# A perceiver kernel: the order of the mixer's loads, the early exponential and the place of two key pieces

## The chip, the cores and the metric

The kernel runs on one core of a Trainium2 chip. The metric is the device time of one execution in microseconds (us). The profile is that of one execution; its times are counted from the start of the profiled span, which is a little shorter than the execution that it belongs to.

## The reference

The kernel is a network of four layers on a latent `x` of 2 x 256 rows of 256 values, with a context `ctx_1024` of 2 x 4096 rows of 256. Each step is a residual of the layer-normed latent:

```python
x = x + _L0_xattn_ref(_layernorm(x), ctx_1024, ...)   # attention over the context
x = x + _L0_attn_ref(_layernorm(x), ...)              # self-attention, 16 heads of 16
x = x + _L0_ffn_ref(_layernorm(x), ...)
x = x + _L1_xattn_ref(_layernorm(x), ctx_1024, ...)   # 16 heads of 64 over the context
x = x + _L1_attn_ref(_layernorm(x), ...)              # the mixer: a scan with W_in, a conv, W_dt, W_out
x = x + _L1_ffn_ref(_layernorm(x), ...)               # int8 weights
x = x + _L2_xattn_ref(ctx_1024, _layernorm(x), ...)   # a long convolution
x = x + _L2_attn_ref(_layernorm(x), ...)
x = x + _L2_ffn_ref(_layernorm(x), ...)               # attention, then routed experts
x = x + _L3_xattn_ref(_layernorm(x), ctx_1024, ctx_1024, ...)
x = x + _L3_attn_ref(_layernorm(x), ...)
x = x + _L3_ffn_ref(_layernorm(x), ...)               # experts, one a row
```

Three parts matter here. The mixer starts with a projection by `W_in`:

```python
zxbcdt = hidden_states @ W_in
z, x, Bm, Cm, dtr = jnp.split(zxbcdt, [...], axis=-1)
```

Each self-attention has a softmax over its scores. And layer 3's attention has one key and one value of 16 for all heads, over the whole context:

```python
kvp = c @ w_kv
k, v = (kvp[..., :D_HEAD], kvp[..., D_HEAD:])
attn_score = jnp.einsum('bhid,bjd->bhij', qh, k) / np.sqrt(D_HEAD)
```

## The kernel before

The 512 rows of the latent lie in four tiles of 128 partitions (`NT` = 4, `x` is 128 x 4 x 256). The layers are methods of one class, emitted one after the other by `perceiver`; a scheduler then sets the order of each engine's instructions from data dependences and what is free, except where a block is wrapped in `in_order(engines)` (L339): there every instruction of a named engine is made to follow the one before it in the program. Memory comes from pools that are opened and closed in the order of the layers. A pool that is opened may lie over one that was closed, and its tiles then wait for the old one. PSUM banks are such a pool too, with the tags mm, tr, acc and dec (`banks`, called in `perceiver` for each layer); a tag with fewer buffers than tiles hands them out in the order in which the tiles are made. Weights come from a pool `wp` of four slots by `weight` (L315 and on), all loaded on SP's queue.

**The start of the mixer.** `l1_attn` (L1464) opens a pool `l1a`. Its first tile is `win` (128 x 2 x 1728 fp32, 1728 KB), loaded at L1474, then the weights wdt and wout, three spread matrices (L1481) and the loads of the next stage in `conv_load` (L1655). `dt2` and `neg_a` (L1486) are small preparations on DVE and ACT; `to_T` (L427) normalizes and transposes `x`; `project` multiplies slices of `win` with it. The tiles `low` and `high` (8 KB per partition each) come later in the same pool. Before the mixer stands the layer-1 attention, which ends with its output matmuls (L1234, `ps_mm` from w_l1x_wo). In the wait for its last sums TensorE works on pieces of layer 3's keys (`ahead_in_drain`, L971 and on).

**Keys ahead of their layer.** A piece of layer 3's keys is two matmuls for 512 context rows (`ahead_key`, two steps of a generator; each fp32 matmul is two records of L971 in the trace, 128 x 512). `ahead_out` (L951) evicts a piece into a tile `ahead_t` (L959 on ACT) and writes it to DRAM as `ahead_k` (L963, 256 KB) from the same engine. `fill_from` and `fill(n)` (L1053) advance such a generator by n steps. `ahead_fetch` (L945) loads what the pieces need: the weights `ahead_l3x_wk`, `ahead_l3x_wv` and the context piece `ahead_piece`. It is called in `perceiver` when the stage int8_and_conv begins. The last two pieces are `ahead_behind`: their context lies in a pool `behind` whose tile `ahead_t` has one buffer, and they are the pieces of the boundary between layers 2 and 3.

**The boundary before layer 3.** `l2_ffn` ends with `experts_in_turn` (L2245): the experts' matmuls, a gather of rows (DVE at L2066) and `bring_back` (matmuls at L359, an addition at L2233). `l3_xattn` then begins with `layernorm` (L373: statistics on DVE, a square root on ACT at L368, the scaling at L384), then the four steps of `fill(4)` and the transposes of `to_T` (L435) in one `in_order(PE)`. The pools of `behind` close after that, and the pool `l3x` with the query's tiles opens. The keys are read back as kT (L2375); `proj_heads` gives qT (L359 with w_l3x_wq); the scores' maxima start with `quad` (L2403) and `mx` (L2407).

**The early exponential.** `self_attention` (L787) is used three times. At L866 it makes a tile `first` and takes an exponential of ones into it, in an `in_order` of PE, DVE and ACT ahead of the loop in which `weights` takes the exponentials of the scores (L840).

Of the kernel before, what the change touches and what calls it, by code (L numbers as in the profile page):

```python
# [11 lines left out]
F32 = mybir.dt.float32  # L12
# [10 lines left out]
P = 128  # L23
# [246 lines left out]
class Perceiver:  # L270
# [518 lines left out]
    def self_attention(self, pool, qT, kT, v, scale, rest=(), fill=None, at=(range(6), range(6, 16), range(16, 22))):  # L789

        nc = self.nc
        z = pool.tile([P, NT, D], F32, name="z")
        with ExitStack() as s:
            one = s.enter_context(self.tc.tile_pool(name="sa_1", bufs=1))  # L800
            pp = s.enter_context(self.tc.tile_pool(name="sa_pt", bufs=14))
            pads = [one.tile([P, 2, 2, P], F32, name=f"mpad{g}") for g in range(4)]
            for pad in pads:
                nc.gpsimd.memset(pad, 0.0)
            zT = [one.tile([P, 4, L], F32, name=f"zTs{b}") for b in range(B)]
            pts, avs = {}, {}

            def maxima(i):

                g, n = divmod(i, 4)  # L810
                b, j = divmod(g, 2)
                rs, t = ((0, 1), (2, 3))[n % 2], n // 2
                lead = pads[g][:, t].rearrange("p c (r w) -> p c r w", w=32)[:, :, :, 0]
                got = [self.bank([P, 2, L]) for _ in rs]
                for c in range(2):
                    for r, ps in zip(rs, got):
                        nc.tensor.matmul(  # L817
                            ps[:, c, :], qT[ts(r, 32), 2 * j + c, ts(2 * b + t, P)], kT[ts(r, 32), 2 * j + c, ts(b, L)],
                            start=True, stop=True,
                        )  # L820
                        yield
                for r, ps in zip(rs, got):
                    nc.vector.tensor_reduce(lead[:, :, r], ps, AX.X, ALU.max, negate=True)

            def weights(i):

                g, n = divmod(i, 4)
                b, j = divmod(g, 2)
                rs, c = ((2, 3), (0, 1))[n % 2], 2 * j + n // 2
                got = [self.bank([P, 2, L], "tr") for _ in rs]  # L830
                for kt in range(2):
                    for r, ps in zip(rs, got):
                        nc.tensor.matmul(  # L833
                            ps[:, kt, :], kT[ts(r, 32), c, ts(2 * b + kt, P)], qT[ts(r, 32), c, ts(b, L)],
                            start=True, stop=True,
                        )
                        yield
                for r, ps in zip(rs, got):
                    pts[c, b, r] = pp.tile([P, 2, L], F32, name="PT", tag="PT")
                    nc.scalar.activation(pts[c, b, r], ps, AF.Exp, scale=scale)  # L840

            def shift(g):
                b, j = divmod(g, 2)
                ps = self.acc([P, 2, 2, P])
                for c in range(2):
                    for t in range(2):
                        nc.tensor.transpose(ps[:, c, t, :], pads[g][:, t, c, :], self.ident)
                q = qT[:, ts(j, 2), ts(b, L)]
                return lambda: nc.vector.tensor_add(q, ps.rearrange("p c t q -> p c (t q)"), q)

            def weigh(g):
                b, j = divmod(g, 2)
                av = self.acc([P, 2, L])
                for c in range(2):
                    for kt in range(2):
                        for r in range(4):
                            h = 4 * (2 * j + c) + r
                            nc.tensor.matmul(
                                av[ts(r, 32), c, :], v[:, 2 * b + kt, h, :], pts[2 * j + c, b, r][:, kt, :],
                                start=kt == 0, stop=kt == 1,  # L860
                            )
                nc.scalar.copy(zT[b][:, ts(j, 2), :], av)

            e = mybir.EngineType
            with self.in_order(e.PE, e.DVE, e.Activation):
                first = self.sm.tile([P, 1], F32, name="first", tag="first")  # L866
                nc.scalar.activation(first, self.ones[:, 0:1], AF.Exp)
                for k in range(16 + 6 + 2):
                    its = []
                    if k < 16:  # L870
                        its.append(maxima(k))
                    if 0 <= k - 6 < 16:
                        its.append(weights(k - 6))
                    then = None
                    if its:
                        self.steps_in_turn(*its)
                    if k < len(rest):
                        rest[k]()
                    for steps, tag, vector in zip(at, ("tr", "acc", "mm"), (False, False, True)):
                        if fill is not None and k in steps:  # L880
                            fill(1, tag, vector)
                    if k % 4 == 0 and 4 <= k <= 16:
                        shift(k // 4 - 1)()
                    if k % 4 == 2 and k >= 10:
                        weigh((k - 10) // 4)
                    if k in (15, 23):
                        b = 0 if k == 15 else 1
                        for t in range(2):
                            self.heads_back(z[:, 2 * b + t, :], zT[b][:, :, ts(t, P)], "acc")
        return z  # L890
# [573 lines left out]
    def l1_attn(self, x):  # L1464
# [5 lines left out]
        with ExitStack() as s:  # L1470
            pool = s.enter_context(self.tc.tile_pool(name="l1a", bufs=1))
            p4 = s.enter_context(self.tc.tile_pool(name="l1a4", bufs=6))
            win = pool.tile([P, KC, 1728], F32, name="win")
            nc.sync.dma_start(win, self.dram["l1a_win"])  # L1474
            wdt = self.weight("l1a_wdt")
            wout = self.weight("l1a_wout")
            mats = {}
            for n in "xbc":
                src = self.dram[f"spread_{n}"]
                mats[n] = pool.tile(list(src.shape), F32, name=f"mat_{n}")  # L1480
                nc.sync.dma_start(mats[n], src)  # L1481
            self.conv_load()
            dt2 = self.sm.tile([P, 4], F32, name="dt2", tag="dt2")
            nc.vector.tensor_scalar_mul(dt2, self.colv("dt_bias"), 2.0)
            neg_a = pool.tile([P, 64], F32, name="neg_a")
# [17 lines left out]
            for k in range(1, 4):  # L1503
                nc.vector.scalar_tensor_tensor(
                    xc, xpad[:, :, k : k + L], self.col("conv_w", k), xc, ALU.mult, ALU.add
                )

            low, high = pool.tile([P, 4, T], F32, name="low"), pool.tile([P, 4, T], F32, name="high")

            def steps_of(j):  # L1510
                ps = self.bank([P, T], "dec")
# [429 lines left out]
    def l2_ffn(self, x):  # L1941
        nc = self.nc
        T = NT * P
        with ExitStack() as s:
# [125 lines left out]
                return add  # L2070

            self.experts_in_turn(unit, n, kept, gather, ways, way, y)
            return y


# [270 lines left out]
    def l3_xattn(self, x, *stacks):  # L2346
# [7 lines left out]


        nc = self.nc
        xn = self.layernorm(x)
        self.fill_from(self.behind_parts)
        with self.in_order(mybir.EngineType.PE):
            self.fill(4)  # L2360
            xnT = self.to_T(xn)
        for stack in stacks:
            stack.close()
        with ExitStack() as s:
# [397 lines left out]
def perceiver(tc, dram, out, col_at, row_at, layers=LAYERS):  # L2762
    with ExitStack() as ctx:
# [6 lines left out]
        for name in layers:  # L2770
            if name == "l0_xattn":
                k.banks(banks, "l0x", 3, 2, 2, 1)
            elif name == "l0_attn":
                banks.close()
                k.banks(banks, "a", 3, 3, 2)
                k.early_open(early)
            elif name == "l1_xattn":

                banks.close()
                early.close()  # L2780
                head.close()
                tern.close()
                k.banks(banks, "l1x", 4, 2, 1, 1)
            elif name == "l1_attn":
                banks.close()
                k.banks(banks, "l1a", 3, 2, 1, 2)
                k.ahead_load(ahead_head)
                k.conv_open(conv)
            elif name == "int8_and_conv":
                banks.close()  # L2790
                k.banks(banks, "l2x", 4, 2, 2)
                k.ahead_fetch()
            elif name == "l2_attn":
                conv.close()
                banks.close()
                k.banks(banks, "c", 3, 3, 2)
                k.l2_keep = keep.enter_context(tc.tile_pool(name="l2f_keep", bufs=1))
                k.ahead_stack, k.behind_stack = ahead, behind
                k.ahead_open(ahead)
            elif name == "l3_xattn":  # L2800

                banks.close()
                k.banks(banks, "l3q", 4, 4, 0)
                k.bank_stack = banks
            elif name == "l3_attn":
                banks.close()
                k.banks(banks, "b", 3, 3, 2)
# [34 lines left out]
```

## Time and profile before

| what | value |
|---|---|
| median of 3 runs | 2532.66 us (2529.35 to 2532.92) |
| the profiled execution | 2533.07 us |
| its span | 2531.3 us |
| mean granted TensorE clock | 0.974 |
| TensorE (PE) busy | 2419.0 us, 96% |
| VectorE (DVE) busy | 1691.5 us, 67% |
| ScalarE (ACT) busy | 1345.3 us, 53% |
| GpSimd (POOL) busy | 911.9 us, 36% |
| DMA | 243.58 MB, 96 GB/s over the span |

The engines are PE (matmul), PEld (its weight loads), DVE, ACT, POOL and SP; a q behind a name is the engine's own queue (semaphores, DMA issues). A line of the timeline has the start, the duration, the engine, the line of the kernel, the operation, out <- in with their shapes, how many instructions were joined, and in brackets how long the engine had stood idle and who released it. The chain of work that ended last is followed back from the last instruction; a window of it lists start, duration and what. In a line of groups, durations are in ns as minimum/median/maximum, then the first and the last start in us.

### The profile page before, as it was taken

To read this page: it belongs to the slowest core of one execution; us is meant where nothing else is said; L and a number is where in the kernel's file an instruction comes from. 1 tells how busy PE (TensorE), PEld (TensorE's weight loads), DVE (VectorE), ACT (ScalarE), POOL (GpSimd) and SP (SyncE) were. 2 spreads that over 40 slices of the span, in tenths; PEclk is the share of its full clock that TensorE was granted. 3 is DMA by queue.
4 is the path that set the end of the run, shared out by engine and by line. 5 is a ranking of instruction groups with operands and counts; after the bars stand their busy time and mean duration, and the time that the engine had idled before them with its cause. 6 is when DMAs were issued, how large, how long until landed. Compare 5 with 4: busy or idle time off the path is not lost.

```text
span 2531.3 us, 51258 instructions
## 1 busy us (share of the span) xinstructions
PE 2419.0 (96%) x20467; PEld 1620.3 (64%) x20469; DVE 1691.5 (67%) x3071; ACT 1345.3 (53%) x2550; POOL 911.9 (36%) x856
## 2 busy tenths in 40 slices
PE   8999999999999999999899989999969999999889
PEld 6865477777766666666533556456926666665678
DVE  5555588888877777777679656444278888845542
ACT  3334576666666666666566323332106777783512
POOL 0420066666655666656459221001101222200010
PEclk9999999999999999999999999989989999998889
DMA  7221433333342222222400102217730000004556
GB/s 298 96 94 69 138 101 93 97 100 99 101 126 68 68 68 69 73 71 85 148 9 1 67 21 96 80 55 279 260 106 2 2 2 2 2 2 167 185 234 216
DMA packets 92637, 243.58 MB, mean 96 GB/s; under 512 B 8072, under 2 KB 23248, under 8 KB 81904
## 3 DMA queue, kind: packets, MB, share of 16 engines
q1 hardware_dynamic: 81088, 219.08, 25.9%
q10 hardware_dynamic: 8784, 13.24, 1.4%
q0 software_dynamic: 2528, 8.00, 0.9%
q8 instruction: 161, 2.64, 0.4%
q14 instruction: 76, 0.62, 0.1%
HBM read 206.87 MB, written 33.42 MB: 95 GB/s over the span
## 4 chain that ended last, share of the span: by engine, by line
PE 88%; DVE 6%; ACT 3%; issue 2%; DMA 1%; DVEq 0%; ACTq 0%; SPq 0%; POOL 0%; POOLq 0%
PE ps_tr L1234 15%; PE ps_mm L359 13%; PE ps_mm L1281 10%; PE acc L1328 9%; PE ps_tr L2462 5%; PE ps_mm L2422 5%; PE ps_tr L2446 5%; PE acc L359 4%; PE ps_tr L359 2%; PE acc L563 2%; PE acc L1611 2%; PE ps_mm L817 2%; PE ps_mm L1234 2%; DVE mx L2407 1%; PE ps_tr L833 1%
## 5 line engine op out<-in xcount | busy, mean ns | idle before, releaser
L1316 POOL TENSOR_TENSOR total<-total,S 128x512 f32<-128x512 f32 x434 | 543.0, 1283 | 227.7 <-ACT S L1305 227.1
L1305 ACT ACTIVATE S<-S 128x512 f32<-128x512 f32 x512 | 304.1, 626 | 209.6 <-DVE S L1302 209.2
L1291 DVE TENSOR_TENSOR most<-ps_mm,most 128x512 f32<-128x512 f32 x448 | 278.1, 683 | 101.0 <-ACT S L1288 101.0
L1302 DVE TENSOR_TENSOR S<-S,ps_dec 128x512 f32<-128x512 f32 x512 | 317.3, 678 | 1.7 <-PE ps_dec L1363 1.7
L2426 DVE TENSOR_REDUCE mx<-ps_mm 128x1 f32<-128x512 f32 x448 | 278.1, 683 | 52.2 <-PE ps_tr L2446 48.2
L1288 ACT COPY S<-ps_mm 128x512 f32<-128x512 f32 x512 | 262.3, 598 | 73.0 <-PE ps_mm L1281 73.0
L2450 ACT ACTIVATE PT<-ps_tr 128x512 f32<-128x512 f32 x476 | 246.8, 601 | 82.4 <-PE ps_tr L2446 79.2
L1234 PEld LDWEIGHTS ps_tr<-w_l1x_wv,ctxT 128*64 128x64 f32 x4096 | 235.5, 137 | 46.3 <-issue 41.7
L1281 PE MATMUL ps_mm<-qT,kT 64*128 64x256 f32 x2048 | 256.6, 389 | 1.8 <-DVE qT L1240 1.8
L1328 PE MATMUL acc<-S,v 128*64 128x256 f32 x2048 | 252.2, 385 | 1.7 <-ACT S L1305 1.0
L1234 PE MATMUL ps_tr<-w_l1x_wv,ctxT 128*64 128x128 f32 x4096 | 248.3, 273 | 0.0
L2446 PE MATMUL ps_tr<-qm,kT 32*128 32x256 f32 x1904 | 240.1, 390 | 0.0
L2422 PE MATMUL ps_mm<-kT,qT 32*128 32x512 f32 x896 | 229.1, 628 | 3.0 <-DVE mx L2407 2.8
L1281 PEld LDWEIGHTS ps_mm<-qT,kT 64*128 64x128 f32 x2048 | 188.5, 186 | 45.5 <-issue 12.0
L1328 PEld LDWEIGHTS acc<-S,v 128*64 128x64 f32 x2048 | 139.5, 136 | 96.3 <-ACT S L1288 33.8
L1234 PE MATMUL ps_tr<-ctxT,w_l1x_wk 128*64 128x512 f32 x800 | 189.6, 593 | 0.0
L2446 PEld LDWEIGHTS ps_tr<-qm,kT 32*128 32x128 f32 x1904 | 172.5, 185 | 16.5 <-issue 6.2
L2471 POOL TENSOR_TENSOR sums<-sums,part 128x256 f32<-128x256 f32 x102 | 73.8, 724 | 250.4 <-ACT part L2470 250.4
L2462 PE MATMUL ps_tr<-PT,v 128*32 128x256 f32 x2048 | 139.4, 385 | 0.0
L2422 PEld LDWEIGHTS ps_mm<-kT,qT 32*128 32x128 f32 x896 | 80.7, 188 | 48.2 <-issue 41.1
L336 DVE COPY v<-ps_tr 128x512 f32<-128x512 f32 x120 | 82.5, 687 | 42.4 <-PE ps_tr L1234 42.4
L1234 PEld LDWEIGHTS ps_tr<-ctxT,w_l1x_wk 128*64 128x64 f32 x800 | 59.7, 137 | 70.5 <-issue 58.7
(573 smaller groups left out, 3859.3 us busy)
## 6 DMA issues: line engine op xcount, KB each, us to landing
ctxT<-in_ctxT SPq DMA_DIRECT2D x144, 512.0 KB, 3.6
w_l2f_gu<-in_l2f_gu SPq DMA_DIRECT2D x16, 1024.0 KB, 6.9
bd_dram<-bd SPq DMA_DIRECT2D x8, 1536.0 KB, 6.0
w_l3f_w<-in_l3f_w SPq DMA_DIRECT2D x11, 1028.0 KB, 10.5
w_l3f_w<-in_l3f_w SPq DMA_DIRECT2D x11, 1024.0 KB, 7.4
ctxT<-in_ctxT SPq DMA_DIRECT2D x8, 1024.0 KB, 6.3
ctx<-in_ctx SPq DMA_DIRECT2D x8, 1024.0 KB, 4.7
ahead_ctx<-in_ctxT SPq DMA_DIRECT2D x8, 1024.0 KB, 5.9
```

The lines of the kernel that those rows point to most:

```text
L359: self.nc.tensor.matmul(out, lhsT, rhs, start=i == 0, stop=i == len(pairs) - 1)
L1234: nc.tensor.matmul(ps[part], a[:, part], b, start=k == 0, stop=k == len(pairs) - 1)
L1281: nc.tensor.matmul(banks[hh, i][:, j, :], k[part, ts(2 * i + j, P)], q[u][part, :], start=True, stop=True)
L1291: nc.vector.tensor_tensor(m, ps, m, ALU.max)
L1302: nc.vector.tensor_tensor(t, t, spread[u][:, hh, :].unsqueeze(1).to_broadcast([P, 2, L]), ALU.add)
L1305: nc.scalar.activation(t, t, AF.Exp)
L1316: nc.gpsimd.tensor_add(tot, tot, t)
L1328: nc.tensor.matmul(av[u][part], vs[:, 2 * i + j, part], got[hh, i][:, j, :], start=g % 8 == 0 and i + j == 0, stop=g % 8 == 7 and i + j == 2,)
L2422: nc.tensor.matmul(ps, qT[rows, 2 * half + c, ts(t, P)], kT[rows, ts(j, 512)], start=True, stop=True,)
L2426: nc.vector.tensor_reduce(mx[:, c, r, j : j + 1], ps, AX.X, ALU.max)
L2446: nc.tensor.matmul(ps[:, i, :], kT[rows, ts(2 * u + i, P)], q[rows], start=True, stop=True)
L2462: nc.tensor.matmul(ps[ts(r, 32), :], v[:, 2 * u + i, :], pt[:, i, :], start=i == 0, stop=i == 1)
```

## The change

Three places change, and nothing that is computed.

- In `self_attention` the tile `first` is replaced by `nought`, made before the loop: it holds the exponential of -1000, that is 0, and it is the bias of the exponentials of the first step of `weights`.
- In `l1_attn` the tiles `low` and `high` are made first, so that `win` lies behind them in the pool, and all loads from `win` to `conv_load` stand in an `in_order` of SP. `ahead_fetch` is called at the end of that block, and no longer in `perceiver` when int8_and_conv begins.
- The two pieces of `ahead_behind` are filled at the end of `l2_ffn`, behind `experts_in_turn` and so in that layer's PSUM banks, in an `in_order` of PE of their own. `l3_xattn` no longer fills them and begins with the layernorm and the transposes alone.

```diff
--- before.py
+++ after.py
@@ -804,6 +804,7 @@
                 nc.gpsimd.memset(pad, 0.0)
             zT = [one.tile([P, 4, L], F32, name=f"zTs{b}") for b in range(B)]
             pts, avs = {}, {}
+            nought = self.sm.tile([P, 1], F32, name="nought", tag="nought")
 
             def maxima(i):
 
@@ -837,7 +838,7 @@
                         yield
                 for r, ps in zip(rs, got):
                     pts[c, b, r] = pp.tile([P, 2, L], F32, name="PT", tag="PT")
-                    nc.scalar.activation(pts[c, b, r], ps, AF.Exp, scale=scale)
+                    nc.scalar.activation(pts[c, b, r], ps, AF.Exp, scale=scale, **({"bias": nought} if i == 0 else {}))
 
             def shift(g):
                 b, j = divmod(g, 2)
@@ -863,8 +864,7 @@
 
             e = mybir.EngineType
             with self.in_order(e.PE, e.DVE, e.Activation):
-                first = self.sm.tile([P, 1], F32, name="first", tag="first")
-                nc.scalar.activation(first, self.ones[:, 0:1], AF.Exp)
+                nc.scalar.activation(nought, self.ones[:, 0:1], AF.Exp, scale=-1000.0)
                 for k in range(16 + 6 + 2):
                     its = []
                     if k < 16:
@@ -1470,16 +1470,19 @@
         with ExitStack() as s:
             pool = s.enter_context(self.tc.tile_pool(name="l1a", bufs=1))
             p4 = s.enter_context(self.tc.tile_pool(name="l1a4", bufs=6))
+            low, high = pool.tile([P, 4, T], F32, name="low"), pool.tile([P, 4, T], F32, name="high")
             win = pool.tile([P, KC, 1728], F32, name="win")
-            nc.sync.dma_start(win, self.dram["l1a_win"])
-            wdt = self.weight("l1a_wdt")
-            wout = self.weight("l1a_wout")
-            mats = {}
-            for n in "xbc":
-                src = self.dram[f"spread_{n}"]
-                mats[n] = pool.tile(list(src.shape), F32, name=f"mat_{n}")
-                nc.sync.dma_start(mats[n], src)
-            self.conv_load()
+            with self.in_order(mybir.EngineType.SP):
+                nc.sync.dma_start(win, self.dram["l1a_win"])
+                wdt = self.weight("l1a_wdt")
+                wout = self.weight("l1a_wout")
+                mats = {}
+                for n in "xbc":
+                    src = self.dram[f"spread_{n}"]
+                    mats[n] = pool.tile(list(src.shape), F32, name=f"mat_{n}")
+                    nc.sync.dma_start(mats[n], src)
+                self.conv_load()
+                self.ahead_fetch()
             dt2 = self.sm.tile([P, 4], F32, name="dt2", tag="dt2")
             nc.vector.tensor_scalar_mul(dt2, self.colv("dt_bias"), 2.0)
             neg_a = pool.tile([P, 64], F32, name="neg_a")
@@ -1504,8 +1507,6 @@
                 nc.vector.scalar_tensor_tensor(
                     xc, xpad[:, :, k : k + L], self.col("conv_w", k), xc, ALU.mult, ALU.add
                 )
-
-            low, high = pool.tile([P, 4, T], F32, name="low"), pool.tile([P, 4, T], F32, name="high")
 
             def steps_of(j):
                 ps = self.bank([P, T], "dec")
@@ -2070,6 +2071,9 @@
                 return add
 
             self.experts_in_turn(unit, n, kept, gather, ways, way, y)
+            self.fill_from(self.behind_parts)
+            with self.in_order(mybir.EngineType.PE):
+                self.fill(4)
             return y
 
 
@@ -2354,11 +2358,7 @@
 
 
         nc = self.nc
-        xn = self.layernorm(x)
-        self.fill_from(self.behind_parts)
-        with self.in_order(mybir.EngineType.PE):
-            self.fill(4)
-            xnT = self.to_T(xn)
+        xnT = self.to_T(self.layernorm(x))
         for stack in stacks:
             stack.close()
         with ExitStack() as s:
@@ -2789,7 +2789,6 @@
             elif name == "int8_and_conv":
                 banks.close()
                 k.banks(banks, "l2x", 4, 2, 2)
-                k.ahead_fetch()
             elif name == "l2_attn":
                 conv.close()
                 banks.close()
```

## The prediction

> **What bounds the kernel now.** I read the shares of the span first, then the chain of work that ended last, then the timelines at the three places that the diff touches. TensorE is busy for 96% of the span and carries most of the chain:
>
> ```profile
> PE 88%; DVE 6%; ACT 3%; issue 2%; DMA 1%; DVEq 0%; ACTq 0%; SPq 0%; POOL 0%; POOLq 0%
> ```
>
> None of the three edits removes work from TensorE. They can only shorten stretches in which it stands still, so each is worth at most the stretch at its place. The first is the start of the mixer (l1_attn), in the chain cut to that window (start, us, what):
>
> ```profile
> 1235.51 6.27 issue
> ...
> 1242.01 9.03 DMA win<-in_l1a_win
> 1251.05 0.14 issue
> 1251.18 5.15 PE ps_mm L359 x8
> ```
>
> TensorE waits for the mixer's input weights `win`. They are issued behind three other loads in SP's queue (start, us, engine, line, what):
>
> ```profile
> 1240.55 0.34 SPq L936 DMA_DIRECT2D ahead_l3x_wk<-in_l3x_wk  x1
> 1240.94 0.43 SPq L936 DMA_DIRECT2D ahead_l3x_wv<-in_l3x_wv  x1
> 1241.42 0.43 SPq L949 DMA_DIRECT2D ahead_piece<-in_ctxT  x1
> 1242.01 0.43 SPq L1474 DMA_DIRECT2D win<-in_l1a_win  x1
> ```
>
> The second is the exponential table. The three early Exp run together at the very start of the span, and the three loads that they are to spare come anyway, in the lines of L867 and L840:
>
> ```profile
> L867 ACT ACTIVATE first<-ones x3: 186/186/202, 2.0 to 2.2; 128x1 f32<-128x1 f32 x3
> ```
>
> ```profile
> L840 ACT ACT_TABLE_LOAD  x3: 1283/1283/1283, 179.6 to 1656.6; - x3
> ```
>
> The third is the boundary before layer 3. TensorE's timeline there shows 3.66 us of idle, then the two key pieces of L971 slow, then the projections:
>
> ```profile
> 1838.32 3.12 PE L359 MATMUL acc<-y_rows,way 128*128 128x256 f32 x12 [1.93 <-ACT y_rows L2327]
> 1845.10 6.72 PE L971 MATMUL ps_tr<-behind_ctx,ahead_l3x_wk 128*128 128x512 f32 x8 [3.66 <-DVE xres L2233]
> 1851.66 1.04 PE L435 MATMUL ps_tr<-ident,xn 128*128 128x128 f32 x8
> 1852.93 7.13 PE L359 MATMUL ps_mm<-xT,w_l3x_wq 128*128 128x512 f32 x16 [0.24 <-ACT xT L331]
> 1862.06 2.00 PE L2403 MATMUL quad<-kT,qT 32*128 32x512 f32 x16 [1.99 <-DVE qT L333]
> ```
>
> The clock column of the stretches says why L971 is slow (0.84 us a record here, 0.45 at 1229.59, where 14 take 6.28 us): 1.00 until 1844, 0.50 from 1845 to 1851.
>
> **Place A, the mixer's weights.** Two things change: `win` lies 16 KB per partition higher, and it is issued ahead of the three loads. I count the address at nothing. The output matmuls of layer 1 end at 1240.60 + 1.08 = 1241.68, and every first write to the newly opened pools starts within 0.8 us of that, whatever it lies over: POOL's h at 1241.89, xpad at 1242.47, and `neg_a`, which lies over score tiles whose readers ended long before:
>
> ```profile
> 1242.17 0.25 ACT L1486 ACTIVATE neg_a<-cols 128x64 f32<-128x64 f32 x1
> 1242.30 0.33 ACTq L963 DMA_DIRECT2D ahead_k<-ahead_t  x1
> 1242.66 1.28 ACT L368 ACT_TABLE_LOAD   x1 [0.24 <-ACT neg_a L1486]
> 1243.95 0.21 ACT L368 ACTIVATE std<-std 128x4 f32<-128x4 f32 x1
> ```
>
> So old pools are released as wholes, at their last reader. With SP free, `win` is issued at about 1241.85, only 0.16 us earlier. The larger part is what no longer travels ahead of it: wk, wv and the piece, 128 + 32 + 512 = 672 KB. The stretches from 1244 to 1250 move 361 to 445 GB/s; at 410 the 1728 KB of `win` and the two 256 KB writes of ahead_k beside it take 5.6 us. Its first packet in the trace comes some 1.2 us after the issue, so it lands at about 1241.85 + 1.2 + 5.6 = 1248.6 and the projections start at 1248.7 instead of 1251.18: **-2.5 us**. Bounds: -0.16 if only the issue moves; -3.4 where the second half of xT is late next (its copy ends at 1247.09 + 0.69 = 1247.78). wdt, wout and l2x_win, so far issued long before, now stand behind `win` in the same queue. wdt (128 KB) is wanted by ps_dec at 1256.33 - 2.5 = 1253.8, 5 us after `win` lands, the three spread matrices at 1264; at 400 GB/s the 768 KB of matrices are 2 us. Those loads are covered, and so are wk, wv and the piece at the end, first wanted at 1546.
>
> **Place B, the exponential table.** `nought` replaces `first` with the same input, `ones`, and the same order on ACT, and its tag has four buffers, so all three can again run at 2 us. The three loads of 1283 ns stay; the bias operand of six Exp (of 591 to 602 ns) I count at nothing, since by the evictions that have one (L959, 665 to 689 ns) it adds 6 x 0.09 = 0.5 us beside a busy TensorE. Sum **0**; bounds +0.5 and 3 x -1.28 = -3.85.
>
> **Place C, the pieces.** Eight matmul records (two keys) leave the place after the residual sum and go, by the order of their banks, right behind the last record of L359 at 1838.32 + 3.12 = 1841.44. There TensorE stands still for 3.66 us at full clock; 8 x 0.45 = 3.6 us fit. That work goes off the path, but it leaves things behind on ACT. Before, ACT's order was the table load for the square root (1838.29, hidden), the root at 1846.94, then the pieces' evictions. They are linked, since `ahead_t` has one buffer:
>
> ```profile
> 1849.70 5.61 DMA ahead_k<-ahead_t
> ```
>
> Now the first eviction comes at 1841.44 + 4 x 0.45 + 0.1 = 1843.3, takes 0.69 and its write is issued at 1844.1. The second eviction must wait for that write, and in a queue that works in order the layernorm's root and its table load wait behind it. The writes of L963 take
>
> ```profile
> DMA to landing us min/median/max: 2.0/2.8/8.5
> ```
>
> The kT loads start at 1844.04 and fill the queues; this boundary's own two writes took 5.61 and 3.9 us. I take 3.9, as the kT loads are only beginning: landing 1848.0, eviction 0.69, issue 0.36, table load 1.28, the root at 1850.4 instead of 1846.94. From the root S on, by the rows: xn at S + 0.45, the first half of xT at xn + 2.64 (layer 1's cold transposes: 1244.40 to 1247.04), projections at S + 3.2, 7.13 us of them, the last eviction and the first quad 0.9 later: S + 11.2 at full clock. TensorE has then been idle since 1845.1. After 1251.18 the clock rose 2.7 us later (mean 0.53 in 1252 to 1254), after 1845.10 6.1 us later (0.95 in 1851 to 1853): half of that is lost, 1.35 or 3.05 us. I take 1.35: quad at S + 12.6 = 1863.0 instead of 1862.06, **+0.9 us**. Bounds: a write of 2.0 us gives -1.0, of 8.5 us +5.5; the slower clock adds up to 1.7 to each. The second write lands by 1852.7 and its reload by 1856.6, so the pad on POOL that waited until 1860.12 is no longer late.
>
> [...]
>
> **The sum.** -2.5 + 0 + 0.9 = -1.6 us against the profiled execution's 2533.07 (span 2531.3 and 1.77 around it): **2531.5**. That execution lies 0.41 above the median of 2532.66, so against the median the change is about -1.2. A measurement of this kernel can tell about 0.2%, 5.07 us, from no change.
>
> **The rivals.**
> - *ACT takes the root first.* If the scheduler puts the root and its load ahead of the second eviction, S stays 1846.94 and quad comes at 1859.5, -2.5: 2533.07 - 5.0 = 2528.1, and up to 1.4 less if the clock holds. For it: the root is ready at 1846.9, about when the write lands; against it: the eviction stands earlier in the program. 0.18.
> - *The address counts.* If the score tiles are released one by one, `win` leaves early and xT's 1247.78 is the floor: -3.4 + 0.9, 2530.6. Against it: neg_a at 1242.17. 0.10.
> - *The edit of the table works*, because the new reader holds the early Exp near its Exp: 1.28 to 3.85 less, 2530.2 to 2527.7. Against it: the row of L867. 0.07.
> - *Slower: a held-up write.* The write of the first piece meets the kT loads as the one of 8.5 us met a busy queue; ACT stands behind it and the root with it. C is then +5.5 and the time 2533.07 - 2.5 + 5.5 = 2536.1. From a landing of 5.5 us on, C eats A; 5.61 was measured in this very traffic, with the loads further on. 0.20, a third of it with a part of A lost too, which is over 0.2%.
> - My forecast has the other 0.45; its own range is 2530 to 2533.
>
> Faster by over 0.2%: half of the first rival, most of the third, and two of them together: 0.2. Slower by over 0.2%: 0.1, with a little for an order of the loads that I do not foresee. Within: 0.7. The range goes from 2526.5 (root first with a warm clock) to 2536.5 (held-up write).
>
> **What would show it.** A: `win` issued at 1241.8 to 1242 with nothing ahead, landing in 6 to 7 us; an issue before 1241.6 would make the address right. B: L867 at 2 us and three loads at L840. C: L971's eight records at 592 ns from 1841.4 less A, the two ahead_t around one write, the table load behind the second, the root later than 1846.94 less A. Wrong would be pieces among the experts' matmuls, a root ahead of the second ahead_t, or a wait for wdt at ps_dec.

## The result

The changed kernel takes 2527.71 us (median of 20 runs, 2522.53 to 2534.66), the kernel before 2532.26 us (20 runs, 2527.36 to 2535.13). The ratio is 0.9984, 95% interval [0.9977, 0.9992]: by the means 4 us less, between 2 and 5.8, and within the 0.2% that the prediction called no change. The profiled execution took 2522.53 us, span 2520.8, and is the fastest of its 20, so the two profiles lie 10.5 us apart where the medians lie 4.6. That gap can't be read as the gain of the edits; the experiments below sort it out.

Lines of the profile after, in the order of the prediction. The shares of the chain are nearly the same:

```profile
PE 89%; DVE 5%; ACT 3%; DMA 1%; issue 1%; SPq 0%; DVEq 0%; ACTq 0%
```

The chain at the mixer's start, and SP's timeline there:

```profile
1238.04 1.11 PE ps_mm L1234 x8
...
1239.28 7.35 DMA win<-in_l1a_win
...
1246.77 5.86 PE ps_mm L359 x8
```

```profile
1239.28 0.34 SPq L1476 DMA_DIRECT2D win<-in_l1a_win  x1
1239.67 0.56 SPq L318 DMA_DIRECT2D w_l1a_wdt<-in_l1a_wdt  x1
1240.28 0.60 SPq L318 DMA_DIRECT2D w_l1a_wout<-in_l1a_wout  x1
```

`win` now leads the queue, is issued 0.16 us behind the end of layer 1's output matmuls (1239.12) and lands after 7.35 us instead of 9.03. The projections come 7.65 us behind that end; before it was 9.50. The early exponential and the table loads of the scores stand where they stood:

```profile
L867 ACT ACTIVATE nought<-ones x3: 186/187/203, 2.0 to 2.2; 128x1 f32<-128x1 f32 x3
```

```profile
L841 ACT ACT_TABLE_LOAD  x3: 1283/1283/1283, 178.0 to 1653.8; - x3
```

TensorE and ACT at the boundary before layer 3:

```profile
1830.87 3.87 PE L359 MATMUL acc<-y_rows,way 128*128 128x256 f32 x16
1834.57 3.60 PE L971 MATMUL ps_tr<-behind_ctx,ahead_l3x_wk 128*128 128x512 f32 x8
1843.03 2.09 PE L435 MATMUL ps_tr<-ident,xn 128*128 128x128 f32 x8 [4.86 <-DVE xn L384]
1845.16 8.68 PE L359 MATMUL ps_mm<-xT,w_l3x_wq 128*128 128x512 f32 x16
1854.67 2.00 PE L2403 MATMUL quad<-kT,qT 32*128 32x512 f32 x16 [0.83 <-issue]
```

```profile
1836.49 0.69 ACT L959 ACTIVATE ahead_t<-ps_tr,cols 128x512 f32<-128x512 f32 x1 [5.05 <-PE ps_tr L971]
1837.21 0.33 ACTq L963 DMA_DIRECT2D ahead_k<-ahead_t  x1
1839.65 0.69 ACT L959 ACTIVATE ahead_t<-ps_tr,cols 128x512 f32<-128x512 f32 x1 [2.47 <-DMA ahead_k<-ahead_t]
1840.37 0.33 ACTq L963 DMA_DIRECT2D ahead_k<-ahead_t  x1
1840.72 1.28 ACT L368 ACT_TABLE_LOAD   x1 [0.39 <-ACT ahead_t L959]
1842.02 0.21 ACT L368 ACTIVATE std<-std 128x4 f32<-128x4 f32 x1
```

The pieces run at full clock (1.00 from 1834 to 1838) right behind bring_back, the second eviction waits for the first write, and the table load and the root stand behind it. The projections are slow (8.68 us against 7.13; the granted clock is 0.50 from 1841.5 to 1848.3), and quad comes 19.9 us behind the last record of bring_back; before it was 20.6. The 1.93 us of idle ahead of the last y_rows matmuls of before is gone, though no edit touches it.

### The profile page after: what moved, and what is told of

Its sections match the earlier page's. It is cut to its first block, busy times and chain, and to the rows that moved or that the text cites. A ratio compares the mean times of both kernels' runs of the same rounds, so it can differ in the third digit from the quotient of the medians.

```text
span 2520.8 us, 51261 instructions
## 1 busy us (share of the span) xinstructions
PE 2414.7 (96%) x20469; PEld 1616.9 (64%) x20469; DVE 1691.1 (67%) x3071; ACT 1346.0 (53%) x2550; POOL 911.6 (36%) x856
## 4 chain that ended last, share of the span: by engine, by line
PE 89%; DVE 5%; ACT 3%; DMA 1%; issue 1%; SPq 0%; DVEq 0%; ACTq 0%
PE ps_tr L1234 15%; PE ps_mm L359 13%; PE ps_mm L1281 10%; PE acc L1328 9%; PE ps_tr L2462 5%; PE ps_mm L2422 5%; PE ps_tr L2446 5%; PE acc L359 4%; PE ps_tr L359 2%; PE acc L563 2%; PE acc L1612 2%; PE ps_mm L818 2%; PE ps_mm L1234 2%; DVE mx L2407 1%; PE ps_tr L834 1%; PE ps_mm L1571 1%
```

## The experiments

Places are compared by their own distances, since a whole execution scatters by several us: from the end of layer 1's output matmuls to the projections and to wout (the first of the matmuls that end the mixer), and from the end of the last record of bring_back to the root and to the first quad. Each time comes with its ratio to the kernel before and the 95% interval.

**The kernel before once more**, unchanged.

> The kernel before, unchanged, once more: how far two sets of runs of one program lie apart, and a second profile of it. My theory: the 2 us of idle ahead of the last y_rows (1836.4 in the first profile) and the 1.5 us at 13 us are chance and are gone or elsewhere; boundary 20.6 us and 9.5 us at the mixer again; ratio 1.0000, within 0.0007. Rival: the stall at y_rows is there again, at the same place, and belongs to the old order.

Ratio 0.9996 [0.9987, 1.0005]. The stall at y_rows is absent, and of the other profiles only the last one below has a longer idle there (0.66 us). It was chance, and from there on it is 2.2 us of the gap between the two profiles. The mixer runs slower here than in the first profile: wout's matmuls come 180.6 us behind layer 1's end, 177.3 in the first.

**The loads alone**: the second part of the change (l1_attn and the moved `ahead_fetch`) on the kernel before.

> The loads' order and address alone, on the kernel before; the table and the pieces stay as they were. My theory: only the order counts. win is issued within 0.2 us of the end of layer 1's output matmuls, the projections start 7.6 us behind that end instead of 9.5 (-1.85, as in the changed kernel), and the boundary before layer 3 keeps its 20.6 us from the last record of bring_back to the first quad. Time: 1.85 less than before, ratio 0.9993, within its interval of no change. Rival, that the 4.5 us of the whole change come from here (the loads of the next stages no longer run beside the mixer): ratio 0.998.

Projections after 7.5 us, wout after 176.8, ratio 0.9986 [0.9977, 0.9995]. Over the six profiles with the old order the projections come after 9.64 us on average and wout after 179.6; over the five with the new one and `win` in one part 7.65 and 177.1. The loads are worth 2.0 us at the projections and 2.5 at the mixer's end. The interval holds both the 0.9993 of the theory and the 0.998 of the rival, so the time doesn't decide between them; the distances do, as the boundary before layer 3 keeps its 20.9 us and the low clock at the third self-attention its 13.7.

**The order without the address**: the tiles `low` and `high` late again.

```diff
-            low, high = pool.tile([P, 4, T], F32, name="low"), pool.tile([P, 4, T], F32, name="high")
             win = pool.tile([P, KC, 1728], F32, name="win")
...
+            low, high = pool.tile([P, 4, T], F32, name="low"), pool.tile([P, 4, T], F32, name="high")
             def steps_of(j):
```

> The changed kernel with the tiles low and high made late again, so that win lies over its old memory; the order of the loads stays. My theory, that old pools are released as wholes: win is issued within 0.3 us of the end of layer 1's output matmuls as in the changed kernel, and the projections start 7.5 to 7.7 us behind that end. Time as the change, ratio 0.9975 to 0.9995. Rival, that the address counts: an issue later than in the changed kernel by 0.5 us or more, and the projections 8 to 9.6 us behind the end.

In its timeline the output matmuls end at 1241.13 + 1.08 = 1242.21 and

```profile
1242.37 0.34 SPq L1475 DMA_DIRECT2D win<-in_l1a_win  x1
```

0.16 us later, as in the changed kernel; projections after 7.62 us, ratio 0.9988 [0.9979, 0.9997]. The address does nothing here.

**win in parts**, on the changed kernel.

```diff
-            win = pool.tile([P, KC, 1728], F32, name="win")
+            cuts = ((1664, 1728), (512, 640), (0, 512), (640, 1664))
+            win = {c: pool.tile([P, KC, c[1] - c[0]], F32, name=f"win{c[0]}") for c in cuts}
...
-                nc.sync.dma_start(win, self.dram["l1a_win"])
+                for c in cuts:
+                    nc.sync.dma_start(win[c], self.dram["l1a_win"][:, :, c[0] : c[1]])
```

> The changed kernel with win in four tiles of columns, loaded in the order in which the projections use them (64, 128, 512, 1024 columns). My theory, that win's landing is what ends last at the mixer's start: the projections start with xT, 5.7 us behind the end of layer 1's output matmuls (7.6 in the changed kernel); the later ones wait for the large parts at most 1 us. Time: 1 to 2 us less than the change, ratio 0.9978. Rival, that short rows make the loads slower or the projections stop at the next part: no gain by the time ps_dec is reached.

```profile
1238.59 1.08 PE L1234 MATMUL ps_mm<-w_l1x_wo,zT 128*64 128x256 f32 x8
...
1245.08 5.48 PE L359 MATMUL ps_mm<-xT,win 128*64 128x512 f32 x8
```

Projections after 5.4 us, with xT and no longer with `win`; wout after 173.8 instead of 177.1. Ratio 0.9969 [0.9957, 0.9981]. What the change left at this place is larger than what it took.

**The pieces alone**: the third part of the change on the kernel before.

> The pieces alone. My theory: the pieces run in the idle time at full clock, the first write lands after 2.4 us, the root comes 7.3 us behind the last record of bring_back (5.5 before) and the first quad 19.9 (20.6 before): -0.7. Time: ratio 0.9997. Rival, that the move is worth more than the boundary shows, since the 2 us stall at y_rows, which the profile of before has and that of after has not, goes with it: -2.9 us, ratio 0.9989, and a profile of this kernel without that stall while the kernels that keep the old place show it.

Root 7.3 us, quad 19.5 us behind bring_back. Over six profiles with the old place quad comes after 20.66 us on average, over four with the new one after 19.67: -1.0. The ratio is 1.0006 [0.9997, 1.0016], so a gain that small doesn't show in the time. The y_rows stall is absent here as in the others, so the rival falls.

**Two buffers for the evicted pieces**, on the changed kernel.

```diff
-        t = pool.tile([P, 512], F32, name="ahead_t", tag="ahead_t")
+        t = pool.tile([P, 512], F32, name="ahead_t", tag="ahead_t", **({"bufs": 2} if pool is getattr(self, "behind", None) else {}))
```

> The changed kernel with two buffers for the evicted pieces at the boundary before layer 3. My theory: the second eviction no longer waits for the first write, the table load ends 1.4 us earlier, the root comes 5.9 us behind the last record of bring_back (7.3 in the changed kernel), the first quad 18.5 (19.9). Time: ratio 0.9978 (0.9984 for the change). Rival, that the root waits for something else (statistics, another load): no change of the root against the changed kernel.

ACT's timeline:

```profile
1842.03 0.69 ACT L959 ACTIVATE ahead_t<-ps_tr,cols 128x512 f32<-128x512 f32 x1 [1.03 <-PE ps_tr L971]
1842.74 0.33 ACTq L963 DMA_DIRECT2D ahead_k<-ahead_t  x1
1843.10 1.28 ACT L368 ACT_TABLE_LOAD   x1 [0.39 <-ACT ahead_t L959]
1844.40 0.20 ACT L368 ACTIVATE std<-std 128x4 f32<-128x4 f32 x1
```

The second eviction waits for its matmuls only; root after 5.84 us, quad after 18.8: the mechanism is shown, 1 us. Yet the ratio is 0.9992 [0.9983, 1.0001], no better than the change: ten of eleven runs lie between 2528.6 and 2531.3, and in its profile the low clock at the third self-attention lasts 13.7 us where the changed kernel had 6.8.

**TensorE kept busy at the boundary**, on the changed kernel.

```diff
                 self.fill(4)
+                ps = self.bank([P, 512], "tr")
+                for _ in range(5):
+                    self.nc.tensor.matmul(ps, self.ones, h2T[:, 0, :], start=True, stop=True)
```

> The changed kernel with five matmuls more (128x512, into a bank that nobody reads) right behind the two pieces of the boundary: TensorE's idle time before the transposes falls from 4.9 to about 0.5 us, with nothing else changed. My theory, that the idle time costs a low clock: the 16 records of the query's projections take 7.1 us instead of 8.2 to 8.7, and the first quad comes 18.3 us behind the last record of bring_back instead of 19.5 to 19.9; ratio 0.9978. Rival, that the clock falls for another reason: 8.2 us or more again.

```profile
1841.99 4.46 PE L2079 MATMUL ps_tr<-h2T,ones 128*128 128x512 f32 x10
1846.66 1.46 PE L435 MATMUL ps_tr<-ident,xn 128*128 128x128 f32 x8 [0.22 <-DVE xn L384]
1848.69 7.13 PE L359 MATMUL ps_mm<-xT,w_l3x_wq 128*128 128x512 f32 x16 [0.57 <-ACT xT L331]
```

7.13 us instead of 8.68 in the changed kernel, quad after 17.9: the low clock had cost 1.5 us (0.3 more of the gain is a write that landed after 2.0 us instead of 2.4; the kT loads come 7.9 us behind bring_back here, not 2.6, so the edit did move something else). Ratio 0.998 [0.9971, 0.9989]; that interval overlaps with the change's, so the gain shows at the place and not in the time.

**The table edit alone**: the first part of the change on the kernel before.

> The exponential alone: nought in the place of first, as the bias of the first exponentials. My theory: nothing moves, the three early Exp at 2.0 to 2.2 us, three table loads at the scores' exponentials, six of these 0.09 us longer; ratio 1.0000 to 1.0002. Rival: the table loads come earlier or two of them vanish, -1.3 to -3.85 us, ratio 0.9985 to 0.9995.

Ratio 0.9988 [0.9979, 0.9997], about 3 us less, with the Exp at 2.0 and three table loads as before. My theory of no effect falls. Beside the kernel before's second profile, TensorE gains 2.8 us between 1658 and 1675, 2.0 of it from 1669 to 1673; up to there the two lie within 0.5 us of each other, and 0.8 more comes at the boundary before layer 3, which the edit doesn't touch. The clock shows why, in the stretches behind the third table load; first that profile, then this one (stretch, us, PE busy, PEld, DVE, ACT, POOL, PEclk, DMA share, GB/s):

```profile
1660.89:1664.31 3.42, 3.12 (x19) 2.31 (x18) 2.19 (x4) 1.75 (x4) 0.00 (x0) 0.50 0.00 0
1664.31:1667.72 3.41, 3.41 (x23) 2.17 (x21) 1.58 (x4) 0.92 (x3) 0.00 (x0) 0.50 0.01 2
1667.72:1671.13 3.41, 3.41 (x26) 2.15 (x30) 1.73 (x3) 1.36 (x3) 0.00 (x0) 0.50 0.02 5
1671.13:1674.55 3.42, 3.42 (x33) 1.63 (x28) 0.00 (x0) 0.59 (x1) 0.00 (x0) 0.51 0.00 0
```

```profile
1660.84:1664.25 3.41, 3.34 (x18) 2.16 (x17) 2.08 (x4) 1.84 (x4) 0.00 (x0) 0.50 0.00 0
1664.25:1667.66 3.41, 3.41 (x22) 2.25 (x20) 1.58 (x3) 0.92 (x3) 0.00 (x0) 0.53 0.01 2
1667.66:1671.08 3.42, 3.41 (x47) 1.97 (x46) 1.97 (x4) 1.61 (x4) 0.00 (x0) 1.00 0.02 5
```

In both the clock falls behind the wait for the table load. In the one it stays low for four stretches of 3.41 us, in the other for two.

**A zero bias, without the early Exp's edit**, on the kernel before.

```diff
+            nought = self.sm.tile([P, 1], F32, name="nought", tag="nought")
+            nc.gpsimd.memset(nought, 0.0)
...
-                    nc.scalar.activation(pts[c, b, r], ps, AF.Exp, scale=scale)
+                    nc.scalar.activation(pts[c, b, r], ps, AF.Exp, scale=scale, **({"bias": nought} if i == 0 else {}))
```

> The kernel before with a zero bias, set by POOL, in the first exponentials of each self-attention; the early Exp stays first, of ones. It has no changed table load, only six exponentials some 0.09 us longer. My theory of the table edit's 2 us (1669 to 1673 in the profile of the table alone): the bias shifts TensorE's first windows behind the table load of the third self-attention, so that its clock is low for two windows of 3.41 us (6.8 us) and not for four (13.7 us): here 6.8 us too, and a ratio of 0.9988 to 0.9995. Rival, that nought itself or chance did it: 13.7 us low behind 1660, ratio 1.0000.

6.8 us, ratio 0.9988 [0.9979, 0.9998], the same as the table edit. Its runs fall in two groups, four at 2523.6 to 2524.7, most others at 2528.8 to 2532.2. So the bias does it, by six evictions of 683 instead of 597 ns (two in each self-attention), and not the table. TensorE gains 2.7 us at the third self-attention here too. Yet the profiled execution, with the short stretch, took 2532.18 us and belongs to the slower group, so this stretch alone doesn't make the groups. And the bias moves the odds and settles nothing: the low stretch is 13.7 us in all four profiles without bias that keep this table load, and with the bias 6.8 in four, 10.2 in one and 13.7 in two.

**The early Exp made late**, on the kernel before.

```diff
-                nc.scalar.activation(first, self.ones[:, 0:1], AF.Exp)
+                nc.scalar.activation(first, qT[:, 0, 0:1], AF.Exp, scale=0.0)
```

> The kernel before with the early Exp read from qT (scale 0), so that it can't run at 2 us: what the table edit would be worth if it did what it says. My theory: the three table loads move ahead of the wait for the first scores, TensorE's wait behind the third falls from 1.63 to about 0.4 us and its clock stays at 1.0 there: -1.3 us three times, and 2 to 4 us of clock at the third, ratio 0.997 to 0.998. Rival, that the loads are covered by other waits: ratio 0.9995 to 1.0000.

```profile
L867 ACT ACT_TABLE_LOAD  x3: 1283/1283/1283, 159.6 to 1628.9; - x3
```

The loads now run ahead of the scores (the third at 1628.9), and there is no low clock at the third self-attention (1.00 in all stretches from 1653 to 1668). Against the kernel before's second profile TensorE gains 1.05, 0.72 and 1.28 us at the three places, where 1.3 each was expected, and 5.4 more up to 1675, in the low stretch that is gone. Ratio 0.9976 [0.9967, 0.9985], 6 us.

**All parts together**: loads in order with `win` in parts, pieces with two buffers, the early Exp from qT.

> All that the experiments point to: the order of the loads with win in four tiles, the pieces in the experts' banks with two buffers, and the early Exp read from qT in place of nought. My theory: the parts lie at different places and add up, projections 5.4 us behind layer 1's end, first quad 18.8 us behind bring_back, no low clock at the third self-attention; 2531.5 - 2.6 - 3.5 - 0.9 - 1.0 - 6 = 2517.5 us, ratio 0.9945. Rival, that the clock's windows of 3.41 us give back part of each: ratio 0.996 or above.

2516.19 us (5 runs, 2514.9 to 2517.11), ratio 0.9943 [0.993, 0.9957]; projections 5.2, quad 18.7, no low clock at the third self-attention. The parts add up.

**And TensorE kept busy at the boundary**, with three matmuls.

> The kernel with all parts together, and three matmuls more behind the two pieces at the boundary, whose result nobody reads: they fill TensorE's idle time up to the transposes of the layernorm. My theory: the clock stays at 1.0 there, the query's projections take 7.1 instead of 8.9 us and the first quad comes 16.9 us behind the last record of bring_back (18.7 without them); 1.8 us less, ratio 0.9936. Rival, that the next clock windows take it back: ratio 0.9943 or above.

2514.97 us (5 runs), ratio 0.9929 [0.9915, 0.9942]; projections 7.13 us, quad 16.87. The intervals of the last two overlap; that it beats the one without the matmuls shows at the place, not in the time.

## Why the prediction was right, and where it failed

- **Place A** held. The issue moved by 0.17 us, the address did nothing (0.10 for that rival), and the order of the loads was what counted; that it is the 672 KB ahead of `win` fits with a landing 1.7 us sooner, but no run takes them away alone. Forecast -2.5; measured -2.0 at the projections, as `win` lands 7.5 us behind layer 1's end where I had 6.9 (all queues together moved 271 to 397 GB/s there, not 410), and -2.5 at the mixer's end. The bare pair of profiles would have hidden it: wout comes 177.3 us behind layer 1's end before, 177.4 after. The first profile of before had run the mixer with 13.7 us of low clock in two stretches, its second one with 20.5. With half of the low clock between the projections and wout taken off, an estimate, wout comes after 173.9 to 174.3 us in all six profiles with the old order and after 171.6 to 172.0 in the five with the new one: -2.3.
- **Place C** had the right mechanism and one term of the wrong size: the first write lands after 2.4 us, not 3.9, since it is issued 0.13 us ahead of the first kT load and not among them (the second write of the kernel with two buffers, which is, takes 5.2). With 2.4 the prediction's own sum gives -0.6; measured -0.7 in the pair and -1.0 over all profiles. The low clock cost the projections 1.55 us in the pair, where the sum had 1.35. In the kernels that moved the pieces the root never came ahead of the second eviction, and the first write never took more than 2.4 us: both rivals fall.
- **Place B** is the step that failed. The reading was right (Exp at 2.0, three loads stay), but the bias operand, which the sum counts at nothing, was not nothing: 0.09 us more on each of two evictions changed how long the clock stays low behind the third load. That is worth 2.8 us in the profile and 3 by the ratio; by estimate about 2 on average, since three of the seven profiles with the bias keep a longer stretch. It is no form of the rival that I had: the table edit doesn't work.
- **The sum.** -2.5, -1.0 and about -2 make -5.5; the time says -4, between -2 and -5.8, and the ratios of the three parts alone multiply to 0.998. The time fell on the forecast's side and inside its wide range, but the 1.6 us forecast lie outside that interval, and 2527.71 lies below the 2530 to 2533 that the prediction gave its own mechanism. It comes close to the 2528.1 of the first rival, which occurred nowhere. Two errors, +0.9 for C and 0 for B, lay on the same side: that the range still held the time is in part luck.

What goes with the end of a low clock shows in the traces, though no run sets it on purpose. Being busy is not enough: at the third self-attention TensorE is busy for the whole 3.41 us in the 11 stretches behind which the clock rises, and also in 13 of the 24 behind which it stays low. The amount of work sorts them. Count in each stretch the columns that the matmuls stream, each weighted by the size of its operand as a share of 128*128, the largest in the traces (32*128 is a quarter). There the clock stays low behind stretches with up to 1490 such columns and rises behind those with 1522 or more. Over all 539 low stretches of the fourteen traces a limit of 1510 sorts 515 rightly, the best limit on busy time 376. How much falls into a stretch depends on where it begins: the clock falls 3.41 to 3.49 us behind the start of the table load in the four profiles without the bias (four low stretches), 3.35 to 3.41 in four with it (two), and 3.76 to 3.83 in the other three (three or four). That 0.09 us matters because a boundary of the stretches lies just there is my reading of these distances; why they keep to so few values is not shown.

## What to carry to other kernels

Compare a place by its own distance from a common event, in several profiles, before a difference of two spans is given to an edit; an unchanged kernel run again showed a stall of 2 us and 7 us of low clock to be chance. When a load is late, ask what travels ahead of it and which part of it is needed first: cutting `win` into columns gave more than its place in the queue (3.3 us at the mixer's end against 2.5). An early instruction must depend on something that is late, or this scheduler takes it to the start, as it did with the exponential at 2.0 us.

## What the runs showed of the hardware

In the profiles of before and of the changed kernel the low stretches of TensorE's clock (0.50) last 3.41 us or a multiple of it, up to 20.5 us, save the last, which is cut off after 2.9 and 2.0 us. In each of the two all others begin and end on one grid of 3.413 us, to within 1.1 ns; its offset from the span's start differs from run to run (1.18 and 1.93 us for two profiles of the kernel before, 1.70 for the changed kernel's). The rises that the prediction took from the first profile of before, 2.7 us behind 1251.18 and 6.1 behind 1845.10, lie on that grid, and so do the falls ahead of them, 2.0 us behind the end of layer 1's output matmuls and 2.9 behind the last record of bring_back. In sum, with some 2 us behind the span's end counted in, the clock was low for 136.0 us in the first profile of before, 155.5 in the second, 124.9 in the changed kernel's and 114.0 in the last one's. Not all of that is on the path: the two executions of the kernel before took 2533.07 and 2532.86 us. But 6.8 us of low clock more or less, where TensorE is the bound, was worth 2.8 us at the third self-attention, as much as any edit of this change.
